# A graph convolution on one core: one more W0 product ahead of its turn, and another order in the last group's sums

## The chip, the cores and the metric

The kernel runs on one core of one Trainium2 chip, so no other core takes part. The metric is the device time of one execution in microseconds (us), and the time of a kernel is the median of its runs. The profile is one more execution, recorded by the hardware profiler; its numbers come from that execution alone.

## The reference, cut to what matters

There are N = 6250 nodes with D = 512 features and E = 100000 edges, sorted by destination. Two graph convolutions follow each other, with a layer norm ahead of each and a residual at the end:

```
norm = -dinv[src] * dinv[dst]                  # dinv = 1/sqrt(degree)
conv(h, W0, W1, b) = h @ W0 + segment_sum(h[src] * norm, dst) @ W1 + b
h   = relu(layernorm(x))
h   = leaky_relu(layernorm(conv(h, W1_0, W1_1, b1)) * gamma + beta)
out = x + conv(h, W2_0, W2_1, b2)
```

Everything is float32. Layer 1's gathers read rows that layer 0 wrote, so layer 1 can gather nothing until layer 0's last block is stored.

## The kernel before, in words

The 100000 edges are cut into 782 **chunks** of 128 edges. One indirect DMA on GpSimd's queue (L393, `gather_to`) fetches the 128 source rows of a chunk (256 KB) into one of 57 slots of the tile `places`, which serve as a ring. Three chunks make a unit, four units a **group**, and there are 66 groups (0 to 65) per layer. The 6250 nodes are cut into 49 **blocks** of 128 (0 to 48; the last has 106).

For a group g, `choose` (L499) builds on VectorE the 0/1 matrix `sel`; `sums` (L519) multiplies it with the gathered chunks. Each of the four units has a quarter q of the result `ps`, 32 of its 128 rows, so that a product uses 32 columns of the array; a full group has 16 products, and in the profile each shows as two passes of float32 (32 passes). ScalarE copies `ps` to `agg` (L530). In a full group the list `todo` goes through the quarters in turn. In the last group (65), whose units have chunks 771 to 774, 774 to 777, 777 to 780 and 780 to 781, the 14 products are sorted by chunk number instead (L525).

Once all groups of block i are summed, `turn(i)` (L584) runs. `own` (L459) transposes the block's own rows by four TensorE transposes (L466), and ScalarE copies the result to `hT` (L468). `place` (L532) moves the sums of the block's groups (three, as a rule) to their rows: for each group VectorE writes a 0/1 matrix `there` (L540) and TensorE makes four products with it (L543, eight passes); the tile pool gives `there` three buffers. VectorE then makes `aT` from the result (L594). `dense` (L598) adds four products `hT` by W0 and four `aT` by W1 in PSUM (L478, 16 passes), and `finish` (L547) does the rest and stores.

The dictionary EARLY (L369) names blocks for which the W0 part is done ahead of time: blocks 46, 47 and 48 at the end of groups 55, 57 and 59. For these `load_early` (two groups before) loads the block's rows into a buffer `pre`, and `early` (L487) transposes, multiplies with W0 and leaves the product plus bias in `pre`; the turn of such a block does no transposes and no W0 products, and `finish` adds `pre`. The pool has as many `pre` buffers as EARLY has entries.

The order of PE, POOL and SP is the program's own (`manual_schedule`, L383). That of VectorE and ScalarE is chosen by the framework's scheduler, but each engine works through its list in order. The loop over groups (L674 on) issues the gathers of a group first, `gather_to(layer, STEP * unit[g] + R)`: 12 gathers ahead of the sums of group g, into the slots that the sums of group g - 1 have read. Then come the turns that are due, the sums of g, the dense part of the due blocks, and the early ones. Turns are due in three groups of every four: block 37 in group 52, 38 in 54, 39 in 55, 40 in 56, none in 53 or 57, block 45 in group 63, 46 and 47 in group 64 and after it, 48 at the end. The gathers of a layer end with group 62.

Of the kernel before, what the change touches and what calls it, by code (L numbers as in the profile page):

```python
# [8 lines left out]
F32 = mybir.dt.float32  # L9
# [10 lines left out]
P = 128  # L20
# [19 lines left out]
def gnn_kernel(  # L40
# [308 lines left out]
    edges.close()  # L349
    unseen = const.tile([1, 1], I32, name="unseen")  # L350
    usual_path(tc, locals())
    stay.close()
    n_unseen = nc.values_load(unseen[0:1, 0:1], min_val=0, max_val=1,
# [6 lines left out]
def usual_path(tc, have):  # L360
# [5 lines left out]
                          "minus unsorted ln dinv sdinv bias1 bias2 gam bet unseen unit N E D NB NC NU NS KD rows places "  # L366
                          "order groups xs sc pick src_lo src_hi p_id dup").split())
    AHEAD = 2
    EARLY = {NB - 3: NS - 11, NB - 2: NS - 9, NB - 1: NS - 7}  # L369
    ACT = mybir.EngineType.Activation  # L370
    R = len(order)
    UN = STEP * P * N / E
# [7 lines left out]
    with ExitStack() as es:  # L380
        pool = es.enter_context(tc.tile_pool(name="main", bufs=2))
# [5 lines left out]
        def zr(t):  # L387
            return places[:, order[t % R], :]
# [58 lines left out]
        def load_h(layer, i, name, bufs):  # L447
            own_h[i] = pool.tile([P, D], F32, name=name, bufs=bufs)
            for lo, hi in parts(rows[i]):
                nc.sync.dma_start(own_h[i][lo:hi], (h_tab if layer else x)[i * P + lo : i * P + hi, :])  # L450

        def load(layer, i):

            if i not in EARLY:
                load_h(layer, i, "h", AHEAD)
            to[i] = pool.tile([P, P], F32, name="to", bufs=AHEAD + 1)
            nc.sync.dma_start(to[i], dup(ndinv_d[i * P : (i + 1) * P], P))

        def own(layer, i):  # L459

            h, r = own_h.pop(i), rows[i]
            if layer == 0:
                nc.scalar.activation(h[:r], h[:r], AF.Relu, bias=ln[:r, 1, i : i + 1], scale=ln[:r, 0, i : i + 1])  # L463
            ps = psum.tile([P, KD, P], F32, name="hT_ps")
            for kc in range(KD):
                nc.tensor.transpose(ps[:, kc, :r], h[:r, kc * P : (kc + 1) * P], ident[:r, :r])  # L466
            hT = pool.tile([P, KD, P], F32, name="hT", bufs=1)
            nc.scalar.activation(hT[:, :, :r], ps[:, :, :r], AF.Copy)  # L468
            return hT

        def load_x(i):
            own_x[i] = pool.tile([P, D], F32, name="xt")
            for lo, hi in parts(rows[i]):
                nc.sync.dma_start(own_x[i][lo:hi], x[i * P + lo : i * P + hi, :])
# [6 lines left out]
        def load_early(layer, i):  # L481
            load_h(layer, i, "pre", len(EARLY))
            pre[i] = own_h[i]
            if layer == 1:
                load_x(i)
# [33 lines left out]
        def sums(g, sel, chunk):  # L519

            n = len(chunk)
            ps = psum.tile([P, D], F32, name="ps")
            todo = [(s, q) for s in range(SPAN) for q in range(n) if s < len(chunk[q])]
            if g == NS - 1:
                todo.sort(key=lambda t: chunk[t[1]][t[0]])  # L525
            for s, q in todo:
                nc.tensor.matmul(ps[q * Q : (q + 1) * Q, :], sel[:, q, s, :], zr(chunk[q][s]), start=(s == 0),  # L527
                                 stop=(s == len(chunk[q]) - 1))
            agg[g] = pool.tile([P, D], F32, name="agg", bufs=3)
            nc.scalar.activation(agg[g][: n * Q], ps[: n * Q], AF.Copy)  # L530

        def place(i, some):  # L532

            r = rows[i]
            if i not in placed:
                placed[i] = psum.tile([P, KD, P], F32, name="aT_ps", bufs=1)
            for g in some:
                m = Q * (unit[g + 1] - unit[g])
                there = pool.tile([P, P], F32, name="there", bufs=3)
                nc.vector.tensor_scalar(there[:m, :r], iota_r[:m, :r], node_of[:m, g : g + 1], -(1.0 + i * P),  # L540
                                        op0=OP.subtract, op1=OP.is_equal)
                for kc in range(KD):
                    nc.tensor.matmul(placed[i][:, kc, :r], agg[g][:m, kc * P : (kc + 1) * P], there[:m, :r],  # L543
                                     start=(g == inside[i][0] and kc == 0),
                                     stop=(g == inside[i][-1] and kc == KD - 1))

        def finish(layer, i, v):  # L547
            r = rows[i]
            v = v[:r]
            if layer == 1:  # L550
                o = pool.tile([P, D], F32, name="t")
                if i in EARLY:
                    nc.vector.tensor_add(o[:r], v, pre.pop(i)[:r])
# [6 lines left out]
            if i < NB - 1:  # L560
                nc.vector.tensor_add(v, v, pre.pop(i)[:r] if i in EARLY else bias1[:r])  # L561
            st = pool.tile([P, 6], F32, name="st")
# [21 lines left out]
        def turn(layer, i):  # L584

            r = rows[i]
            if layer == 1 and i not in EARLY:
                load_x(i)
            if i + AHEAD < NB:
                load(layer, i + AHEAD)  # L590
            hT = None if i in EARLY else own(layer, i)
            place(i, [g for g in inside[i] if i < NB - 1 or g == NS - 1])
            aT = pool.tile([P, KD, P], F32, name="aT", bufs=1)
            nc.vector.tensor_tensor(aT[:, :, :r], placed.pop(i)[:, :, :r],  # L594
                                    to.pop(i)[:, None, :r].to_broadcast([P, KD, r]), op=OP.mult)
            return hT, aT
# [71 lines left out]
        for layer in range(2):  # L668
# [5 lines left out]
            for g in range(NS):  # L674
# [16 lines left out]
                if g == NS - 2:  # L691
                    for k, (hT, aT) in due:
                        dense(layer, k, hT, aT)
                    due = []
                sums(g, *(chosen if g == NS - 1 else choose(g)))
                if layer == 0:
                    if g == 0:
# [17 lines left out]
                if g == NS - 2:  # L715
                    chosen = choose(NS - 1)
                    if layer == 0:
                        r = rows[NB - 1]
                        started[NB - 1] = psum.tile([P, D], F32, name="u_ps")
                        nc.tensor.matmul(started[NB - 1][:r], ident[:r, :r], pre[NB - 1][:r], start=True, stop=False)  # L720
                    while inside[i].stop < NS:
                        dense(layer, i, *turn(layer, i))
                        i += 1
                    assert i == NB - 1
                    place(i, inside[i][:-1])
# [323 lines left out]
```

## Time and profile before

| what | us |
|---|---|
| median of 3 runs (2527.57 to 2532.97) | 2531.47 |
| the profiled execution | 2509.83 |
| its span, first to last instruction | 2508.0 |
| PE busy, matmuls | 1948.0 |
| POOL busy (gathers) | 1496.6 |
| DVE busy | 691.2 |
| ACT busy | 377.3 |
| granted TensorE clock, mean | 0.885 of full |

Layer 0's groups lie between about 120 us and 1310 us of the span, layer 1's between 1310 us and the end. In the profile a line gives an engine, a kernel line and a tile; the time in brackets is idle time of the engine before it, with what the profile takes for its end. "remote" and "issue" mean that the profile names no instruction. A matmul's end is modelled, and passes on different quarters of the array overlap, so the mean of a pass (649 ns at L527) is not its share of the time.

### The profile page before, as it was taken

How to read it: one execution, taken by the hardware profiler on the slowest of the kernel's cores; microseconds unless marked ns; L12 is line 12 of the kernel's file. 1: busy time of each engine (PE TensorE's matmuls, PEld its weight loads, DVE VectorE, ACT ScalarE, POOL GpSimd, SP SyncE). 2: the span in 40 equal slices, each digit the busy share in tenths (PEclk: the TensorE clock that was granted, in tenths of full speed). 3: DMA queues.
4: the chain of work that ended last, by engine and by line, in shares of the span. 5: the costliest groups of instructions: out<-in, count | busy, mean ns of one | idle time of the engine just before them, and what ended most of it. 6: DMA issues, size and time to landing. Idle time of an engine off the chain costs nothing.

```text
span 2508.0 us, 24149 instructions
## 1 busy us (share of the span) xinstructions
PE 1948.0 (78%) x9101; PEld 913.8 (36%) x9101; DVE 691.2 (28%) x1381; ACT 377.3 (15%) x694; POOL 1496.6 (60%) x1577
## 2 busy tenths in 40 slices
PE   5617788688888888887874568887888888688888
PEld 4414343243334334333430233333333333343344
DVE  8923223232324223323340011111111111111221
ACT  8724111111111111112110000000000000000000
POOL 4175666666666666665507566666666666666660
PEclk8757899899999999999996679998998989889999
DMA  9395677767677677776627567677676777677770
GB/s 341 102 336 152 213 228 217 213 209 223 211 220 256 208 223 222 215 224 214 188 70 214 178 201 225 208 229 221 218 226 212 221 212 221 211 214 236 220 225 28
DMA packets 198947, 527.08 MB, mean 210 GB/s; under 512 B 31864, under 2 KB 46019, under 8 KB 198822
## 3 DMA queue, kind: packets, MB, share of 16 engines
q0 software_dynamic: 125120, 410.09, 53.7%
q1 hardware_dynamic: 73702, 115.36, 13.3%
q8 instruction: 73, 1.20, 0.2%
q14 instruction: 52, 0.43, 0.1%
HBM read 474.06 MB, written 51.27 MB: 209 GB/s over the span
## 4 chain that ended last, share of the span: by engine, by line
PE 67%; issue 17%; another core or an unknown queue 5%; DVE 5%; POOL 3%; DMA 2%; ACT 1%; SPq 0%; POOLq 0%; DVEq 0%; ACTq 0%
PE u_ps L478 26%; PE ps L527 25%; PE aT_ps L543 13%; POOL places L393 3%; PE hT_ps L466 2%; DMA places<-tab,sidx 1%; DVE hi L256 1%; DVE lo L256 1%; DVE places L404 0%; DVE places L405 0%; ACT agg L530 0%; PE both_ps L262 0%; PE u_ps L433 0%; PE hT_ps L433 0%
## 5 line engine op out<-in xcount | busy, mean ns | idle before, releaser
L393 POOL DMA_INDIRECT places<-tab,sidx x1504 | 1421.8, 945 | 844.3 <-issue 395.5
L527 PE MATMUL ps<-places,sel 128*32 128x512 f32 x4168 | 734.2, 649 | 158.8 <-issue 108.9
L543 PE MATMUL aT_ps<-there,agg 128*128 128x128 f32 (+2 forms) x2320 | 381.7, 313 | 207.4 <-issue 191.8
L543 PEld LDWEIGHTS aT_ps<-there,agg 128*128 128x128 f32 (+1 forms) x2320 | 340.2, 222 | 245.7 <-issue 224.0
L527 PEld LDWEIGHTS ps<-places,sel 128*32 128x32 f32 x4168 | 165.9, 117 | 647.6 <-issue 585.7
L515 DVE TENSOR_TENSOR sel<-dlx,nodes_ps 128x512 f32<-128x512 f32 (+3 forms) x134 | 89.7, 671 | 804.9 <-remote 513.6
L530 ACT ACTIVATE agg<-ps 128x512 f32<-128x512 f32 (+1 forms) x132 | 78.7, 596 | 1206.2 <-remote 632.1
L478 PE MATMUL u_ps<-w,hT 128*128 128x512 f32 (+1 forms) x392 | 189.7, 616 | 25.4 <-issue 15.9
L478 PE MATMUL u_ps<-places,hT 128*128 128x512 f32 (+1 forms) x392 | 185.7, 611 | 14.7 <-ACT hT L468 7.6
L478 PE MATMUL u_ps<-w,aT 128*128 128x512 f32 (+1 forms) x392 | 181.1, 596 | 13.8 <-issue 9.8
L478 PE MATMUL u_ps<-places,aT 128*128 128x512 f32 (+1 forms) x392 | 177.9, 593 | 6.6 <-issue 4.2
L540 DVE TENSOR_SCALAR there<-iota_r,node_of 128x128 f32<-128x128 f32 (+1 forms) x290 | 84.1, 293 | 340.0 <-remote 184.3
L478 PEld LDWEIGHTS u_ps<-w,hT 128*128 128x128 f32 (+1 forms) x392 | 71.7, 192 | 140.6 <-issue 121.0
L478 PEld LDWEIGHTS u_ps<-places,hT 128*128 128x128 f32 (+1 forms) x392 | 70.7, 190 | 127.3 <-issue 119.4
L478 PEld LDWEIGHTS u_ps<-w,aT 128*128 128x128 f32 (+1 forms) x392 | 73.1, 189 | 114.3 <-issue 108.9
L478 PEld LDWEIGHTS u_ps<-places,aT 128*128 128x128 f32 (+1 forms) x392 | 73.9, 189 | 101.7 <-issue 98.7
L594 DVE TENSOR_TENSOR aT<-aT_ps,to 128x512 f32<-128x512 f32 (+1 forms) x98 | 67.3, 687 | 150.9 <-PE ps L527 117.5
L393 POOL DMA_INDIRECT places<-in_x_dram,sidx x44 | 44.2, 1005 | 90.3 <-ACT places L407 58.8
L468 ACT ACTIVATE hT<-hT_ps 128x512 f32<-128x512 f32 (+1 forms) x98 | 58.1, 593 | 246.7 <-PE hT_ps L466 69.8
L561 DVE TENSOR_TENSOR u_ps<-u_ps,bias 128x512 f32<-128x512 f32 x46 | 32.2, 700 | 190.7 <-PE u_ps L478 86.1
L555 DVE TENSOR_TENSOR u_ps<-u_ps,bias 128x512 f32<-128x512 f32 x46 | 32.1, 699 | 183.2 <-PE u_ps L478 92.1
L463 ACT ACTIVATE h<-h,ln 128x512 f32<-128x512 f32 x46 | 37.2, 812 | 256.4 <-issue 131.0
(138 smaller groups left out, 963.7 us busy)
## 6 DMA issues: line engine op xcount, KB each, us to landing
places<-tab,sidx POOLq DMA_INDIRECT x1504
tab<-t SPq DMA_DIRECT2D x48, 256.0 KB
h_tab<-g SPq DMA_DIRECT2D x48, 256.0 KB
xt<-in_x_dram SPq DMA_DIRECT2D x48, 256.0 KB
out_dram<-t SPq DMA_DIRECT2D x48, 256.0 KB
h<-in_x_dram SPq DMA_DIRECT2D x46, 256.0 KB
h<-h_tab SPq DMA_DIRECT2D x46, 256.0 KB
places<-in_x_dram SPq DMA_DIRECT2D x4, 1792.0 KB
```

Source lines behind the costliest of these rows:

```text
L256: nc.vector.tensor_tensor(t, s[:, g * 2 * GJ : (g + 1) * 2 * GJ].rearrange("p (j s) -> p j s", s=2)[:, :, None, :] .to_broadcast([EP, GJ, ...
L393: nc.gpsimd.indirect_dma_start(out=zr(t), out_offset=None, in_=x if layer == 0 and t < RAW else tab[layer], in_offset=bass.IndirectOffsetO ...
L463: nc.scalar.activation(h[:r], h[:r], AF.Relu, bias=ln[:r, 1, i : i + 1], scale=ln[:r, 0, i : i + 1])
L466: nc.tensor.transpose(ps[:, kc, :r], h[:r, kc * P : (kc + 1) * P], ident[:r, :r])
L468: nc.scalar.activation(hT[:, :, :r], ps[:, :, :r], AF.Copy)
L478: nc.tensor.matmul(u_ps[:r], hT[:, kc, :r], w[:, kc, :], start=(start and kc == 0), stop=(stop and kc == KD - 1))
L515: nc.vector.tensor_tensor(sel[:, q : q + k, :w, :], of, node[:, q : q + k, None, :].to_broadcast([P, k, w, Q]), op=OP.is_equal)
L527: nc.tensor.matmul(ps[q * Q : (q + 1) * Q, :], sel[:, q, s, :], zr(chunk[q][s]), start=(s == 0), stop=(s == len(chunk[q]) - 1))
L530: nc.scalar.activation(agg[g][: n * Q], ps[: n * Q], AF.Copy)
L540: nc.vector.tensor_scalar(there[:m, :r], iota_r[:m, :r], node_of[:m, g : g + 1], -(1.0 + i * P), op0=OP.subtract, op1=OP.is_equal)
L543: nc.tensor.matmul(placed[i][:, kc, :r], agg[g][:m, kc * P : (kc + 1) * P], there[:m, :r], start=(g == inside[i][0] and kc == 0), stop=(g ...
L594: nc.vector.tensor_tensor(aT[:, :, :r], placed.pop(i)[:, :, :r], to.pop(i)[:, None, :r].to_broadcast([P, KD, r]), op=OP.mult)
```

## The change

A fourth block, 45, is added to EARLY; its W0 part is done at the end of group 53, and its rows are loaded at the end of group 51. With that the pool makes four `pre` buffers. In the last group the products keep the order of a full group (through the quarters in turn) but for chunks 780 and 781, which still come last. The pool's buffers for `there` go from three to two.

```diff
-    EARLY = {NB - 3: NS - 11, NB - 2: NS - 9, NB - 1: NS - 7}
+    EARLY = {NB - 4: NS - 13, NB - 3: NS - 11, NB - 2: NS - 9, NB - 1: NS - 7}
...
             if g == NS - 1:
-                todo.sort(key=lambda t: chunk[t[1]][t[0]])
+                todo.sort(key=lambda t: max(chunk[t[1]][t[0]], NC - 3))
...
-                there = pool.tile([P, P], F32, name="there", bufs=3)
+                there = pool.tile([P, P], F32, name="there", bufs=2)
```

## The prediction, made before the changed kernel had run

> **What bounds the kernel now.** I read the page first, for what repeats.
>
> ```profile
> L393 POOL DMA_INDIRECT places<-tab,sidx x1504 | 1421.8, 945 | 844.3 <-issue 395.5
> L527 PE MATMUL ps<-places,sel 128*32 128x512 f32 x4168 | 734.2, 649 | 158.8 <-issue 108.9
> ```
>
> No engine is full (PE 78%, POOL 60%), so I read the timeline of POOL next. Gathers start 1.25 us apart (945 ns and 0.30 idle), 12 to a group, and about once in 12 POOL stops:
>
> ```profile
> 1929.07 0.95 POOL L393 DMA_INDIRECT places<-tab,sidx  x1 [0.30 <-issue]
> 1930.32 0.95 POOL L393 DMA_INDIRECT places<-tab,sidx  x1 [0.30 <-issue]
> 1933.98 0.95 POOL L393 DMA_INDIRECT places<-tab,sidx  x1 [2.72 <-remote]
> ```
>
> Most stops are 2.2 to 3.0 us. Four groups take 4 x 12 x 1.25 + 4 x 2.4 = 69.6 us, and the timeline repeats every 70 us through the middle of both layers. The stop is for a ring slot, free when the previous group's sums have read it. PE's clean work in four groups is 3 blocks of 10.2 us (16 passes at L478 7.06, transposes 0.44, place 2.68) and four sums of 3.6: 45 us. So POOL with its stops sets the pace there, and PE has some 25 us of slack in 70, which stutter and handshakes eat. The timelines of PE and of VectorE in the same stretch show them:
>
> ```profile
> 1923.71 2.84 PE L543 MATMUL aT_ps<-there,agg 128*128 128x128 f32 x24
> 1926.48 1.90 PE L527 MATMUL ps<-places,sel 128*32 128x512 f32 x11
> 1928.65 2.70 PE L527 MATMUL ps<-places,sel 128*32 128x512 f32 x4 [0.26 <-issue]
> ```
>
> ```profile
> 1924.21 0.69 DVE L556 TENSOR_TENSOR t<-u_ps,xt 128x512 f32<-128x512 f32 x1
> 1932.16 0.29 DVE L540 TENSOR_SCALAR there<-iota_r,node_of 128x128 f32<-128x128 f32 x1 [7.26 <-remote]
> 1933.62 0.29 DVE L540 TENSOR_SCALAR there<-iota_r,node_of 128x128 f32<-128x128 f32 x1 [1.17 <-remote]
> ```
>
> PE's first eight passes of the place end at 1924.6 and free a `there` buffer, but VectorE, idle, hears of it at 1932.2: while POOL gathers, PE's completions reach the others late, often only when POOL has stopped. It is no single case; the answer on line L540 for layer 1 between 1430 and 2440 us says what VectorE waited for there:
>
> ```profile
>   remote: 96.1, 29
>   PE ps L527: 46.3, 16
> ```
>
> With the smaller rows (15.5 and 13.5) that is 171 us of 63 waits. Now nobody suffers: with three buffers the `there` that VectorE makes is for the next block.
>
> After the last gather (2441 us in layer 1, 1245 in layer 0) nothing of this is left. The timeline of all engines at the end:
>
> ```profile
> 2457.35 0.60 PE L466 MATMUL hT_ps<-ident,h 128*128 128x128 f32 x4
> ...
> 2458.89 0.28 DVE L540 TENSOR_SCALAR there<-iota_r,node_of 128x128 f32<-128x128 f32 x1
> ...
> 2464.13 3.70 PE L478 MATMUL u_ps<-places,hT 128*128 128x512 f32 x8
> ...
> 2467.66 3.60 PE L478 MATMUL u_ps<-places,aT 128*128 128x512 f32 x8
> ...
> 2489.26 5.40 PE L527 MATMUL ps<-places,sel 128*32 128x512 f32 x28
> ```
>
> PE runs without a gap, and every us taken from it is a us of the end. VectorE's `there` starts 0.2 us after the eight passes that free it (2458.7).
>
> **The change, part by part.** Sums are against the profiled 2509.83 us (span 2508.0); the runs' median is 2531.47, 0.9% above. I add the difference in us to the median.
>
> *W0 of block 45 leaves the tail.* Transposes, 2457.35 to 2457.78: 0.43. W0 passes, 2464.13 to 2467.66: 3.53. Together 3.96 us a layer, 7.9 us in two. What is late next is PE itself: VectorE's `aT` of that block (2460.66) is hidden by the sums (2460.6 to 2464.1). Its load (L450) leaves the turn of block 43.
>
> *It arrives in group 53.* The like of it, block 46 in group 55, takes 4.88 us of PE in layer 1 (2342.71 to 2347.59), 0.74 of it idle for ScalarE's `hT`. In group 53 POOL is in mid-stream; the sums end at 2294.5, and ScalarE's next start is 2304.54, after a wait of 19.44 us. So the W0 passes start near 2305, when today PE still waits for that same ScalarE (`agg`, 2304.54) in block 38's place. PE falls 5 to 7 us behind. POOL wants the sums of 54 at 2319 and gets them (begun near 2314), but at group 56, where PE today starts at 2350.8 and POOL wants it at 2351.9, I find about 2 us lost. In layer 0 the stop at 1152.23 is 6.86 us, so PE is late already; there I allow 0 to 3. Together 0 (other handshakes swallow it) to 5, taken: 2 us.
>
> *VectorE, ScalarE, SP.* One add more per layer (L494 instead of none; in layer 1 two instead of one), 0.7 us at 28% load, beside PE: nothing; without cover 1.4 us. SP issues `pre` and, in layer 1, `xt` (0.4 us each) at the end of group 51. Block 45 holds one of two `xt` buffers until group 53, so block 38's load queues behind it, with SP's later loads; all are for later turns. Nothing; if uncovered, 2 us.
>
> *Order of group 65.* By the chunk lists the quarters now go 0 1 2, 0 1 2, 0 1 2, 0 1 3, 2, 3: mostly three side by side, not four. A step from pass to pass is 0.43 us, a last pass 0.59. A full group's 3.64 us is 8 steps; the old order's 5.40 is 12. In the new one quarters 0 to 2 need 8 steps, and the last product of quarter 3 follows chunk 780's: 10 steps, 9 x 0.43 + 0.59 = 4.46. Gain 0.94 a layer. The Trainium skill ("TensorE: Matmul & The Clock Gate", Part 3[...]) says that matmuls start and end strictly in program order. Counted so, each pass in turn, the old order would need 19 steps (8.3 us) and the new 15, a gain of 1.7; but 8.3 is not the row's 5.40. I take 0.94 (bounds 0.9 and 1.8), 1.9 us for two layers. All chunks have landed long before: the last gather is issued 48 us ahead of group 65.
>
> *`there` with two buffers.* This is the step with the largest unknown. A place needs three; the third is now the buffer of its first, so inside each place PE waits for PE -> VectorE -> PE. In the tail this costs nothing (0.2 + 0.28 us against 0.89 of the second eight passes). Under the gathers the trace shows the same signal with today's buffers. Block 22 above: `there` complete at 1932.45, third part of the place due at 1925.5, PE waits 7 us; sums at 1933.5 instead of 1926.48; their first product (1.02) and 0.3 for the signal bring POOL to 1934.8 instead of 1933.98, +0.8. Block 40 (`there` 2353.64, place's third part due 2349.8): POOL at 2356.3 instead of 2354.10, +2.2, the most in any such place, since PE needs 2.2 us after the stop has let the signal through. Block 37: PE waits 2.6 us, POOL loses nothing. Walking 86 turns so, PE waits 2.4 us on average (over 200 in all), but POOL is moved in only 20, by 0.1 to 2.2, 28 us in sum. Bounds: 0 (the signal comes sooner when PE stands still) and 86 x 2.2 = 189. I take 28, the walk's own sum.
>
> Against this stands a rule of the skill ("SBUF — State Buffer", SBUF: two separate sides): engine and DMA sides of SBUF cannot contend, and TensorE never waits. If gathers then could not delay PE's signals at all, every place would be like the tail's, the cost 0 and the change a gain of 8 us. The rows of 0.2 us without gathers and 7.3 with them say otherwise, whatever path it is that is shared; I go by the rows.
>
> Sum: -7.9 - 1.9 + 2 + 28 = +20 us: 2530 profiled, 2551 against the median.
>
> **The rivals.** A change under 0.2% (5 us) can't be told from none here.
>
> *The pace is POOL's and absorbs the third `there`* (faster): -9.8 + 2, about 2524. For it: 66 of 86 turns move POOL by nothing, and PE saves stutter when its sums follow a stop (3.64 us instead of 9). Against it: the slack of the third turn in four is under 5 us, and three waits of 2.4 add up. Chance 0.25.
>
> *Cost and gain cancel* (about 8 us of waits): 2531. 0.14.
>
> *Locked* (much slower): PE, later with each wait, frees its buffer later in POOL's run, where the signal only comes with the stop (released 5.4 us into a run it took 3.1 us, at 8 to 9 us mostly 5 to 8), and one turn in four groups loses the full 2.2: 30 x 2.2 = 66, plus irregular ones; with -8, about 2590 and up. 0.18.
>
> *My sum*, some turns and not others: 2551, own range 2537 to 2570. 0.43.
>
> **How the numbers follow.** Faster 0.25, within 0.2% 0.14, slower 0.61. The likeliest gives 2551. The range goes down to 2520, the first rival with its early work free, and up to 2600, into the locked case.
>
> **What would show it.** In the tail: no L466 and no `hT` passes in group 63, and group 65's 28 passes in 4.4 to 4.5 us. In the middle: PE idle ahead of the last eight passes of a place, with DVE L540 as its end, and POOL's stops longer than 3 us in turns' groups, cycles over 70 us. If the cycle stays at 70 us, the `there` step is wrong; if it lengthens without idle time in the places, it is another cause, such as a new order of VectorE's list.

## The result, and the profile after

| | us |
|---|---|
| before, median of 4 runs (2519.07 to 2532.97) | 2529.52 |
| after, median of 4 runs (2595.73 to 2609.64) | 2604.89 |
| after, the profiled execution (span 2599.2) | 2600.98 |

The change made the kernel slower: ratio 1.0303, 95% interval 1.0276 to 1.033, or 75 us. The profiled executions are 91 us apart, since the one of before lies 20 us under its median; what follows accounts for those 91.

Two groups of the page of before that had not been shown, the place products and `there`:

```profile
L543 PE MATMUL aT_ps<-there,agg 128*128 128x128 f32 (+2 forms) x2320 | 381.7, 313 | 207.4 <-issue 191.8
...
L540 DVE TENSOR_SCALAR there<-iota_r,node_of 128x128 f32<-128x128 f32 (+1 forms) x290 | 84.1, 293 | 340.0 <-remote 184.3
```

The page after, with the lines of gathers, sums, place and `there` (busy us and mean ns between the bars, then idle us ahead):

```profile
L393 POOL DMA_INDIRECT places<-tab,sidx x1504 | 1425.8, 948 | 936.7 <-issue 391.6
L527 PE MATMUL ps<-places,sel 128*32 128x512 f32 x4168 | 665.9, 704 | 82.8 <-issue 42.1
L543 PE MATMUL aT_ps<-there,agg 128*128 128x128 f32 (+2 forms) x2320 | 405.1, 325 | 402.2 <-issue 308.6
L540 DVE TENSOR_SCALAR there<-iota_r,node_of 128x128 f32<-128x128 f32 (+1 forms) x290 | 82.8, 287 | 394.4 <-remote 235.5
```

A gather still takes 948 ns and is issued no slower, but POOL is idle 92 us longer before its gathers (844.3 to 936.7). TensorE's idle time has moved: ahead of the place products (L543) it grew by 195 us, ahead of the sums (L527) it shrank by 76. From the start of group 3's sums to that of group 63's, layer 0 went from 1040.9 to 1093.2 us (+52.3) and layer 1 from 1043.4 to 1086.3 (+42.9), 95 us together; the ends of the layers became shorter. So the loss stands in the middle, where gathers run.

The answer on line L540 after, layer 1, 1470 to 2540 us of the span; the last lines say who waited for `there`. Before, one wait of 0.2 us stood there.

```profile
  remote: 110.7, 41
...
who waited for it (us, times):
  PE aT_ps L543: 42.5, 12
```

Here is one turn in both kernels, from timelines of PE, POOL and DVE (start, duration, then idle time in brackets). Before:

```profile
1578.63 2.84 PE L543 MATMUL aT_ps<-there,agg 128*128 128x128 f32 x24
1581.41 1.91 PE L527 MATMUL ps<-places,sel 128*32 128x512 f32 x13
```

```profile
1584.32 0.95 POOL L393 DMA_INDIRECT places<-tab,sidx  x1 [0.30 <-issue]
1588.05 0.95 POOL L393 DMA_INDIRECT places<-tab,sidx  x1 [2.78 <-remote]
```

```profile
1586.20 0.29 DVE L540 TENSOR_SCALAR there<-iota_r,node_of 128x128 f32<-128x128 f32 x1 [6.38 <-remote]
```

TensorE runs the 24 passes of the place in one piece. Its first eight free a `there` at about 1579.7, but VectorE hears of it only at 1586.20, 0.9 us after POOL's last gather has ended (1585.27) and POOL stands still. That `there` is for the next block, so nobody minds. Such a turn after:

```profile
1629.70 1.95 PE L543 MATMUL aT_ps<-there,agg 128*128 128x128 f32 x16
1637.06 2.05 PE L543 MATMUL aT_ps<-there,agg 128*128 128x128 f32 x8 [5.41 <-issue]
1639.04 4.92 PE L527 MATMUL ps<-places,sel 128*32 128x512 f32 x32
```

```profile
1636.63 0.29 DVE L540 TENSOR_SCALAR there<-iota_r,node_of 128x128 f32<-128x128 f32 x1 [5.74 <-remote]
```

```profile
1635.43 0.95 POOL L393 DMA_INDIRECT places<-tab,sidx  x1 [0.30 <-issue]
1641.23 0.95 POOL L393 DMA_INDIRECT places<-tab,sidx  x1 [4.86 <-PE ps L527]
```

Now 16 passes run, and the last eight need the third `there`, whose buffer the first eight freed at about 1630.8. VectorE hears of it at 1636.63, 0.25 us after POOL's last gather ended (1636.38). The trace also records the semaphore, the counter by which TensorE tells of its work: the one that `there` waits for rises at 1636.61, although the eight passes ended at 1630.76, and `there` starts 0.02 us behind it. So the signal is late, and not VectorE. Only then, inside POOL's stop, come `there` (0.29), the last eight passes, and at 1639.04 the sums for which POOL waits. Before, these sums had begun at 1581.41, ahead of the stop. It is a circle: POOL stops because the sums are late, the sums wait for a signal, and in this turn the signal comes when POOL has stopped.

TensorE is also slow in this stop. The view of two stretches of time has the granted clock in the third column from the right, for the first 16 passes and then from `there` to POOL's next gather:

```profile
1629.70:1631.65 1.95, 1.95 (x18) 1.76 (x16) 1.16 (x2) 0.60 (x1) 1.36 (x2) 1.00 0.74 193
1636.63:1641.23 4.60, 4.17 (x20) 2.38 (x24) 1.46 (x4) 0.00 (x0) 0.00 (x1) 0.50 0.49 186
```

Behind its wait of 5.41 us TensorE works at half its clock. From the start of the eight passes to that of the sums it takes 1.98 us, and from there to POOL's next gather 2.19. In the stop of before that ends at 1152.23 the sums came late too, but TensorE had not waited ahead of these passes, and has its full clock:

```profile
1149.90:1152.23 2.33, 2.33 (x23) 1.31 (x25) 1.17 (x3) 0.00 (x0) 0.00 (x0) 1.00 0.83 264
```

There the same two steps take 0.99 and 1.32 us. The difference is 1.86 us, most of the 2.08 by which this stop grew (2.78 to 4.86).

Counted from POOL's timeline (idle over 0.6 us between gathers, from chunk 100 of each layer on): before, 129 stops with 319.6 us, six of them over 4 us; after, 136 with 406.4 us, 28 over 4. That is +86.8 of the 95 us that the middles gained. By group: those with number 1 modulo 4 (9, 13, 17, ...) went from 80.6 to 150.8 us, 2.88 to 5.39 for each of 28; the three other kinds together by +16.6. The gathers of such a group wait for sums behind the last turn of the three that follow each other. In 26 of the 28 stops over 4 us the last eight passes had waited more than 1 us; TensorE's clock was at half for 81% of the time of these stops. In 20 of the 28, both of the two steps above took the longer time. Over all 28 the steps took 44 us more than 0.99 and 1.32 each.

### The profile page after: what moved, and what is told of

The parts are those of the page before. It is cut to its first block, busy times and chain, and to the rows that moved or that the text cites. A ratio compares the mean times of both kernels' runs of the same rounds, so it can differ in the third digit from the quotient of the medians.

```text
span 2599.2 us, 24147 instructions
## 1 busy us (share of the span) xinstructions
PE 1908.0 (73%) x9101; PEld 916.8 (35%) x9101; DVE 694.8 (27%) x1383; ACT 379.8 (15%) x694; POOL 1500.7 (58%) x1577
## 4 chain that ended last, share of the span: by engine, by line
PE 58%; issue 16%; another core or an unknown queue 14%; DVE 6%; POOL 2%; DMA 1%; ACT 1%; SPq 0%; POOLq 0%; ACTq 0%; DVEq 0%
PE u_ps L478 23%; PE ps L527 21%; PE aT_ps L543 12%; POOL places L393 2%; PE hT_ps L466 2%; DMA places<-tab,sidx 1%; DVE lo L256 1%; DVE hi L256 1%; DVE u_ps L561 0%; DVE st L564 0%; PE both_ps L262 0%; ACT agg L530 0%; DVE there L540 0%; DVE u_ps L555 0%
## 5 line engine op out<-in xcount | busy, mean ns | idle before, releaser
L393 POOL DMA_INDIRECT places<-tab,sidx x1504 | 1425.8, 948 | 936.7 <-issue 391.6
L527 PE MATMUL ps<-places,sel 128*32 128x512 f32 x4168 | 665.9, 704 | 82.8 <-issue 42.1
L543 PE MATMUL aT_ps<-there,agg 128*128 128x128 f32 (+2 forms) x2320 | 405.1, 325 | 402.2 <-issue 308.6
L543 PEld LDWEIGHTS aT_ps<-there,agg 128*128 128x128 f32 (+1 forms) x2320 | 356.7, 231 | 445.3 <-issue 397.3
L527 PEld LDWEIGHTS ps<-places,sel 128*32 128x32 f32 x4168 | 151.7, 127 | 518.1 <-issue 468.4
L478 PE MATMUL u_ps<-w,hT 128*128 128x512 f32 (+1 forms) x392 | 195.9, 637 | 30.6 <-ACT hT L468 15.3
L540 DVE TENSOR_SCALAR there<-iota_r,node_of 128x128 f32<-128x128 f32 (+1 forms) x290 | 82.8, 287 | 394.4 <-remote 235.5
L262 PE MATMUL both_ps<-hi,lo 125*128 125x196 bf16 x400 | 46.4, 279 | 30.4 <-DVE hi L256 30.0
```

Of the source, the lines that this page charges most:

```text
L262: nc.tensor.matmul(both_ps, hot[0][:, j, :], hot[1][:, j, :], start=(g == 0 and j == 0), stop=(g == EJ // (2 * GJ) - 1 and j == GJ - 1))
L393: nc.gpsimd.indirect_dma_start(out=zr(t), out_offset=None, in_=x if layer == 0 and t < RAW else tab[layer], in_offset=bass.IndirectOffsetO ...
L478: nc.tensor.matmul(u_ps[:r], hT[:, kc, :r], w[:, kc, :], start=(start and kc == 0), stop=(stop and kc == KD - 1))
```

## The experiments

Theory A: the loss is the third `there` buffer's alone, by signals that come late while POOL issues gathers. Rivals: W0 in group 53, the new order of the last group, or a new order of VectorE's list. The kernels ran on five chips, on which the kernel before took quite different times: 2529.81, 2102.95, 2517.86, 2102.16 and 2101.11 us. Each kernel is therefore compared only with the runs of before that were made beside it.

**First chip (before: 2529.81 us).**

The kernel before with two `there` buffers and nothing else:

```diff
-                there = pool.tile([P, P], F32, name="there", bufs=3)
+                there = pool.tile([P, P], F32, name="there", bufs=2)
```

> The kernel before with one edit: two buffers of there instead of three. Theory A (the third there of each place waits for PE's signal, which is late under the gathers): it carries most of the 75 us of the change, so 2529 + 60 to 85, and POOL's every fourth stop is near 5 us instead of 2.5, as in the changed kernel. Rival B (the early W0 part of block 45 pushes PE behind in groups 53 to 60, and everything after it waits): within 0.3% of before. Rival C (VectorE's new order does it): between the two, without idle time ahead of the last part of a place.

Measured: 2604.54 us, ratio 1.0282 (1.024 to 1.0324). POOL's stops: 27 over 4 us, 416.1 us in all. One buffer carries the whole loss, and its long stops are of the same kind: the eight passes had waited more than 1 us in 25 of the 27, and the two steps took 42 us more than at the full clock's times.

The changed kernel with three `there` buffers. They no longer fitted beside the fourth `pre`, so a small tile (`diff`) was moved into the pool of an earlier stage, which is given back before the groups:

```diff
-    diff = const.tile([P, P], F32, name="diff")
...
+    diff = ep.tile([P, P], F32, name="diff")
...
-                there = pool.tile([P, P], F32, name="there", bufs=2)
+                there = pool.tile([P, P], F32, name="there", bufs=3)
...
```

> The changed kernel with three buffers of there again; to make room the 512-byte tile diff, needed only at the start, goes into a pool that is freed (the general path, which does not run, makes its own). Theory A: the loss is gone; what is left is the tail's gain of 2 x (3.96 + 1.74) = 11 us less what group 53 to 60 lose, so 2518 to 2535. Rival B: still 50 us or more slower than before, with the longer stops in groups 53 to 60 alone.

Measured: 2518.76 us, ratio 0.9953 (0.9938 to 0.9968), with four stops over 4 us. This is faster than both kernels: the two other edits are a gain of 11 us. The late signals are still there (in layer 1 117.6 us of 29 "remote" waits at L540), but no place product waits for `there`, and the mean granted clock is 0.898 instead of the 0.847 of both kernels with two buffers. With two buffers the gain of 11 us doesn't show: the loss is 75 us with the other edits and without them. The interval of the second figure is about 11 us to either side.

The kernel before with the new order of group 65 alone:

```diff
-                todo.sort(key=lambda t: chunk[t[1]][t[0]])
+                todo.sort(key=lambda t: max(chunk[t[1]][t[0]], NC - 3))
```

> The kernel before with the new order of the last group's products alone. The changed kernel's profile has that group at 3.66 us in both layers where before has 5.40. Both theories: 3.5 us less, 2526, about 0.14%, at the edge of what five rounds tell; group 65 at 3.66 us. If instead group 65 stays at 5.40, the order did nothing by itself.

Measured: 2526.05 us, ratio 0.999 (0.9971 to 1.001). The 3.8 us are within what can't be told from none; in its trace group 65 takes 3.66 us instead of 5.40, which is 3.5 us in two layers.

The kernel before with block 45 in EARLY and the old order (three `there` buffers, `diff` moved):

```diff
-    EARLY = {NB - 3: NS - 11, NB - 2: NS - 9, NB - 1: NS - 7}
+    EARLY = {NB - 4: NS - 13, NB - 3: NS - 11, NB - 2: NS - 9, NB - 1: NS - 7}
```

> The kernel before with block 45 in EARLY alone: three buffers of there (diff moved as in the run before), the old order in the last group. Theory A: between 8 us faster and 8 us slower, 2521 to 2537, since the tail gives 7.9 us and groups 53 to 60 take some back; the regular stops stay 2.2 to 3.0 us. Rival B: 40 us or more slower.

Measured: 2524.76 us, ratio 0.9977 (0.9961 to 0.9993): -5.0 us. The two parts add up to the 11 us of both together within their intervals.

**Second chip (before: 2102.95 us).** One buffer and four, in the kernel before (`bufs=1`, `bufs=4` for `there`):

> The kernel before with one buffer of there: every part of a place but the first must wait for PE's signal about the part before it, two such waits in each place instead of one with two buffers. If the wait for the late signal is the cause, the second wait comes on top wherever POOL is gathering again or still: 130 to 220 us over before, 2660 to 2750, and POOL's long stops in more than one group of four. If two buffers cost their 75 us by some other order of VectorE's list, one buffer need not cost more than about 90 us.

Measured: 2110.12 us, ratio 1.0042 (1.0027 to 1.0056). A plain miss.

> The kernel before with four buffers of there. By theory A the third there is already one block ahead with three, so a fourth gains nothing: within 0.2% of before. If lateness of the signal costs something even with three buffers, this gains 5 us or more.

Measured: 2101.94 us, ratio 0.9995 (0.9987 to 1.0003).

The runs of this chip stand at another level: from chunk 100 on POOL has no stop over 0.6 us in either trace. Gathers follow each other every 1.25 us through a whole layer, and TensorE waits for their data (230 us at L527 in the page of four buffers, 220 of it for `places`). Next, the kernel before without the gathers behind the first 57 chunks of each layer, with three and with two buffers; the sums then work on rows of other chunks, so that most of the aggregation is left out, and only the time is of use:

```diff
-            for t in range(gathered, min(end, NC)):
+            for t in range(gathered, min(end, NC, R)):
```

> The kernel before, but only the first 57 gathers of each layer are issued (gather_to stops at the ring's size); the sums read whatever the slots hold, so the aggregation is left out in effect. Nothing waits for POOL then. PE's clean work, 15 us a block, sets the pace: about 2530 - 2 x 320 = 1890 us, 1800 to 2000.

> The same without gathers, with two buffers of there. Theory A (the signal is late because of the gathers, 0.2 us without them): within 15 us of the run with three buffers. If a third there costs its wait whatever POOL does: 60 us or more above it.

Measured: 1708.38 us (1708.12 to 1712.25) and 1710.55 us (1708.44 to 1711.13). The level was lower than I expected, since I had worked it out from runs at 2530; the third buffer is worth nothing without gathers, but here, as the run with one buffer says, it is worth little with them too. So the pair had to be run at the other level.

**Third chip (before: 2517.86 us).**

> Two chips have shown two levels of the kernel before: 2530 us and 2103 us. Theory A (the late hand-over of `there` is a matter of the chip that takes the program): where the kernel before is near 2530 us, the changed kernel takes 2595 to 2615 (ratio 1.026 to 1.034); where it is near 2103 us, the changed kernel takes 2095 to 2110 (ratio 0.996 to 1.003), because there one buffer fewer costs nothing. Rival B (the loss is a cost of the program's own, the same on any chip, and one buffer's +7 us on the faster chip had another cause): ratio 1.025 or more at either level.

Measured: 2563.82 us, ratio 1.0193 (1.015 to 1.0235), 46 us: slower, but less than on the first chip, and below the range expected. POOL's stops: 19 over 4 us. In layer 0 most of them stand in groups of number 1 modulo 4, as on the first chip; in layer 1 the longest (9.4 to 9.7 us) stand in groups 12, 20, 32, 40 and 44, of number 0.

> One buffer of `there`, the rest as before. Theory A: where the kernel before is near 2530 us, the loss grows with each buffer taken away: above 2650 us (two buffers cost 75 us; with one buffer each chunk's mask waits for the products of the chunk before, about 290 times in the run, 0.5 us or more late each time). Where it is near 2103 us: 2105 to 2116, as measured there. Rival B (what counts is only that the third turn of four stalls once in four groups, which one buffer does not make worse): 2595 to 2630 at the 2530 level.

Measured: 2683.35 us, ratio 1.0651 (1.0612 to 1.069), 165 us. The answer on L540 for layer 1, 1470 to 2540 us, with one buffer:

```profile
who waited for it (us, times):
  PE aT_ps L543: 105.0, 29
  PEld aT_ps L543: 29.0, 6
```

The wait grew with the buffers taken away (42.5 us with two, in the changed kernel on the first chip), and so did the loss. 36 stops are over 4 us, and the mean granted clock is 0.808.

> The kernel before without the gathers behind the first 57 chunks of each layer (the rest of the aggregation's data left out). Theory A (TensorE's instructions and signals are slowed only while gathers are issued): 1700 to 1720 us on either chip, with a granted clock above 0.95, so a ratio near 0.675 where the kernel before is near 2530 us and near 0.813 where it is near 2103 us. Rival B (the slower chip is slower by its clock or memory, whatever the gathers do): 1950 to 2100 us where the kernel before is near 2530 us.

> The kernel of the run before this one with two buffers of `there` instead of three. Theory A: within 5 us of it on either chip, since without gathers no signal is late. Rival B (two buffers cost TensorE's own time): 40 to 75 us longer than it where the kernel before is near 2530 us.

Measured: 1764.51 us (1763.51 to 1765.84) and 1763.44 us (1762.57 to 1765.07). Without gathers this chip is 3% slower than the second (1708), not the 20% that lie between 2518 and 2103, and above the 1720 expected at most; and the missing buffer costs nothing. The answers on L540 (1200 to 2520 us), with three and with two buffers, name no late signal at all:

```profile
  PE aT_ps L543: 29.0, 46
```

```profile
  PE aT_ps L543: 29.0, 46
```

That is 0.63 us at a time, about what is left of eight passes (0.89 us) after VectorE's own 0.28. With the gathers, in the run with one buffer on the same chip, "remote" stood at 119.0 us of 43 waits. The gathers, their issue or their traffic, make the signals late on this chip.

**Fourth chip (before: 2102.16 us).** Two kernels were to say in which turns the loss stands: the changed kernel (with `diff` moved), and in it one more buffer for the third `there` of every third turn alone, or (`i % 3 != 1`) of the two others:

```diff
-                there = pool.tile([P, P], F32, name="there", bufs=2)
+                alone = i % 3 == 1 and g == some[-1]
+                there = pool.tile([P, P], F32, name="there_x" if alone else "there", bufs=1 if alone else 2)
```

> The changed kernel with two buffers of `there`, but with a buffer of its own for the third `there` of one turn in three: that of the last of three turns that follow each other in four groups (block number 1 modulo 3). Where the kernel before is at 2510 to 2535 us and the changed one 45 to 75 us above it: theory A (locked: the stops over 4 us stand behind just these turns, and carry the loss) expects that at least two thirds of the loss are gone: ratio to before 1.000 or below up to 1.008, and the count of GpSimd's stops over 4 us in the middle of the layers back from 19 to 28 to below 12. Rival B (each turn costs its own third by waiting for the signal, and the long stop is only where it adds up) expects one third gone: ratio 1.010 to 1.020. Where the kernel before is near 2103 us: ratio 0.995 to 1.002 by both.

> The same the other way round: the third `there` has a buffer of its own in the two other turns of three, and not in the last of the row. Theory A: most of the loss stays, ratio to before 1.010 to 1.030, stops over 4 us 15 or more. Rival B: two thirds of the loss gone, ratio 1.000 to 1.010. Near 2103 us: ratio 0.995 to 1.002 by both.

> The changed kernel once more, as the measure of the two runs before this one on the same chip. Where the kernel before is at 2510 to 2535 us: ratio 1.018 to 1.034. Where it is near 2103 us: theory A (no late signal there, so one buffer fewer costs nothing and the tail's gain of some 10 us remains) 0.994 to 1.000; rival (the loss is the program's own on any chip) 1.018 or more.

> The changed kernel with three buffers of `there` (the small tile `diff` moved to make room). By all theories the tail's gain alone: ratio to before 0.993 to 0.998 at either level; above 1.000 would say that the third buffer does not undo the loss.

| kernel | us | ratio to before |
|---|---|---|
| third buffer in the last turns | 2094.21 | 0.996 (0.9946 to 0.9974) |
| third buffer in the other turns | 2094.27 | 0.9967 (0.9953 to 0.9982) |
| the changed kernel | 2094.18 | 0.9961 (0.9947 to 0.9976) |
| the changed kernel, three buffers | 2094.79 | 0.9969 (0.9958 to 0.998) |

All four are the same. The first two tell nothing on the turns here; the third tells most: on this chip the very change that lost 3% is a gain of 8 us. From its timelines of DVE and PE:

```profile
1640.92 0.28 DVE L540 TENSOR_SCALAR there<-iota_r,node_of 128x128 f32<-128x128 f32 x1
```

```profile
1639.81 2.84 PE L543 MATMUL aT_ps<-there,agg 128*128 128x128 f32 x24
1642.59 3.64 PE L527 MATMUL ps<-places,sel 128*32 128x512 f32 x32
```

The first eight passes end at 1640.87, and the third `there` starts 0.05 us later, where the turn of the first chip took 5.87. The 24 passes run in one piece with two buffers, although POOL issues gathers beside them all the time. The mean granted clock is 0.939.

**Fifth chip (before: 2101.11 us).** The two kernels for the turns once more:

> As in the run with the third `there` buffer for the last of three turns: where the kernel before is at 2510 to 2535 us, theory A (the loss stands in that turn) a ratio of up to 1.008 and fewer than 12 of GpSimd's stops over 4 us; rival B (each turn its third) 1.010 to 1.020. Near 2103 us 0.995 to 0.998 by both.

> As in the run with the third buffer for the two other turns: where the kernel before is at 2510 to 2535 us, theory A a ratio of 1.010 to 1.030 and 15 or more stops over 4 us; rival B 1.000 to 1.010. Near 2103 us 0.995 to 0.998 by both.

Measured: 2093.2 us, 0.9959 (0.9945 to 0.9973), and 2093.24 us, 0.9964 (0.995 to 0.9978). Again a chip on which nothing is late. In which turns the loss stands was therefore not settled by a run.

## Why the prediction was wrong, step by step

**W0 of block 45 leaves the tail: right.** After, layer 1's end shows no W0 passes behind group 63's sums:

```profile
2555.18 3.64 PE L527 MATMUL ps<-places,sel 128*32 128x512 f32 x32
2558.75 3.70 PE L478 MATMUL u_ps<-places,aT 128*128 128x512 f32 x8
...
2580.45 3.66 PE L527 MATMUL ps<-places,sel 128*32 128x512 f32 x28
```

From the sums of group 63 to those of 64 the time fell from 17.8 to 14.4 us in layer 1 (18.4 to 15.0 in layer 0): 3.4 of the 3.53 us of the passes; the transposes' 0.43 lies ahead of it.

**It arrives in group 53 at +2 us: not contradicted.** With three buffers the whole edit gave -5.0 us where the two terms gave -5.9. After, the W0 passes wait 7.24 us for ScalarE's `hT`, much as foreseen, and then take 5.33 us, where those of the tail took 3.70:

```profile
2382.46 5.33 PE L478 MATMUL u_ps<-places,hT 128*128 128x512 f32 x8 [7.24 <-ACT hT L468]
```

**Order of group 65: right in sign, too small.** The 28 passes take 3.66 us (shown above), eight steps of a full group, not 4.46 and ten. I had let the last product of quarter 3 wait for that of chunk 780, another quarter. In the trace three passes start together in the first four steps and four in the last four, so no step is added behind the eight. The gain is 5.40 - 3.66 = 1.74 a layer, 3.5 us in all instead of 1.9. That this is close to the 1.7 which strict order would have given is chance: strict order put the new list at 15 steps, some 6.6 us, and the row says 3.66.

**`there` with two buffers, +28 us: the step that failed, by its size.** The way it would lose was as written: the last eight passes wait for VectorE's `there`, POOL's stop grows, the cycle of 70 us gets longer. The size was not: the run with only this edit lost 75 us. What the walk had too small is the chain inside a stop. It took 1.05 us from a finished `there` to the sums and 1.32 (first product 1.02, signal 0.3) from there to POOL's next gather, the times of TensorE at its full clock, and its cap of 2.2 per turn is made of the same pieces. But TensorE comes to these steps out of the wait that the missing buffer causes, and then has half its clock: in the turn shown they took 2.12 and 2.19, together 4.31 instead of 2.37. In the run with only this edit, the steps took 42 us more in its long stops than at the full clock's times, which is about the 47 us between 28 and 75. That share is an estimate from the trace: no run held the clock up. The number of turns was nearer, 20 against 28 stops over 4 us.

The walk also took each turn at its place in the trace of before, one by one. What I read from the trace as a link left out: once a turn's sums start in a stop, the same turn of the next four groups meets POOL's run at the same place again, and is late again. This is the rival that I called locked ("one turn in four groups loses the full 2.2", about 2590 and up, chance 0.18), and the trace of the changed kernel looks like it: in the 28 groups of number 1 modulo 4 the stops are longer by 2.5 us each, 70 us. But it isn't shown that the loss is tied to that turn: the runs for it were made where nothing is late, and on the third chip long stops stood elsewhere too. What is shown is that the buffer makes the loss, and that it stands in POOL's stops, +86.8 us in sum.

**The rival in which POOL's pace absorbs the third `there`** (2524) did happen, on the chips of the other level: there the change gained 8 us, where the terms without `there` gave -7.8. There POOL doesn't stop in the middle of the layers, and the signals are not late.

**The rule weighed there** (the Trainium skill, "SBUF — State Buffer", SBUF: two separate sides) would have given a gain of 8 us. Where the kernel before takes 2518 to 2531 us, the rows decide against it as a guide to this time: on the third chip 119.0 us of late signals with gathers, none without. On the fourth chip its number came true. The rule speaks of SBUF's ports; what delays the signals, no run here shows, and so neither agrees with it nor breaks it.

## What to carry to other kernels

A buffer that is never waited for in the trace can still be what keeps a late signal off the path: before taking one away, find when its release is heard, not when it is freed. If that is when another engine stands still, and that engine waits for the work behind the buffer, count the full length of the new chain in every stop, at the clock that the trace shows behind such a wait, and not only the walk over today's places. And when memory is short, look for another tile to move first: here moving 64 KB in all (`diff`, 128 x 128 of float32) turned 3% of loss into 0.5% of gain on the first chip.

## What the runs showed that I had not expected

The kernel before took 2518 to 2531 us on some chips and 2101 to 2103 on others. At the higher level TensorE's signals come to VectorE up to 7 us late while POOL issues gathers, and POOL stops about once in 12 gathers; at the lower one `there` starts 0.05 us after the passes that free its buffer, POOL never stops in mid-layer, and the data of the gathers is what TensorE waits for. Without gathers the two levels are 3% apart (1764 to 1708 us), so about 360 of the 415 us between them come only with the gathers. Whether it is the chip or what else it was doing in that hour can't be told from these runs.
